# Layer 3 attention: stacked 64-row score matmuls, and one exponential in sixteen on VectorE

## The chip, the cores and the metric

The kernel runs on one core of a Trainium2 chip. The metric is device time in microseconds (us). TensorE is called PE here, its weight loads PEld, ScalarE is ACT, VectorE is DVE, GpSimd is POOL, and SP is the queue that issues the DMAs.

## What is computed

Four layers run over x of shape (2, 128, 64, 64), each `x = x + layer(groupnorm(x))`. Only the last one, attention over 4096 pixels with 8 heads of 16 channels, is changed:

```python
# layer 3, on xf = groupnorm(x) as (B=2, C=128, S=4096)
q, k, v = proj(wq, bq), proj(wk, bk), proj(wv, bv)      # each (B, 8, 16, S)
a = einsum('bhcq,bhck->bhqk', q, k) / sqrt(128)
a = softmax(a, axis=-1)
o = einsum('bhqk,bhck->bhcq', a, v).reshape(B, C, h, w)
x = x + o
```

## The kernel before, in words

Line numbers are those of the kernel before; a program prints the functions below. Layers 0 to 2 end at 2222 us of the trace and are not touched. Layer 3 (`_layer3`, L1963) works through four groups, one for each image b and half t of the heads: four heads at a time. A group has 8 query blocks (qb) of 512 queries, and a block has 32 key tiles (kt) of 128 keys. One (qb, kt) is called a step here; there are 4 x 8 x 32 = 1024.

In a step `scores` (L2102) multiplies keys by queries for the four heads. A head stands on 32 rows: 16 rows of rounded keys, 16 rows of what the rounding lost, and the queries twice (`q[0]` rounded, `q[1]` the rest). The first pass (n = 0) puts four matmuls of 32 rows side by side on the array, one for each head, and the second pass (n = 1) adds four more. Heads 0 and 1 fill one PSUM tile of two banks (p = 0), heads 2 and 3 another (p = 1). The pool has three such tiles (`spp`, bufs=3), used in turn. ACT then takes the exponential of each tile, 128 x 1024 (L2112), into an SBUF tile `weights`, of which there are eight. `multiply` (L2121) takes the weights of two steps earlier by the values, four matmuls of 128 rows and 32 columns, each recorded as two, and adds into a PSUM tile `ps_acc`, which there are two of. After the 32nd key tile `done` divides by the sum and adds the residual on DVE (L2144 to L2152), with four small DMAs for the residual (L2141) and four for the output (L2154).

Queries and keys of a group (L2030 to L2046) are made in eight chunks of 512 columns, values (L2056, L2063) in eight portions of four key tiles. `work` makes those of the next group as a generator, of which `attend` takes one piece at kt 4, 12 and 20 of each block; those of the first group are made during its own first block, one piece at every second step. So a side matmul stands in PE's queue between a step's multiply and the next step's scores. The instructions of PE, DVE, ACT and POOL keep the program's order (`_in_order`); SP's order is chosen by the scheduler. At the end of a group the two waiting steps are multiplied before the next group's first scores.

Of the kernel before, what the change touches and what calls it, by code (L numbers as in the profile page):

```python
# [10 lines left out]
F32 = mybir.dt.float32  # L11
# [1277 lines left out]
F32R = mybir.dt.float32r  # L1289
ENGINES = (  # L1290
# [672 lines left out]
def _layer3(ctx, tc, X, l3, cst, out, worst, here):  # L1963
# [6 lines left out]
    pp = ctx.enter_context(tc.tile_pool(name="f3_p", bufs=8))  # L1970
# [16 lines left out]
    def folded(b, got):  # L1987

        x = X[:, b, :]
        if b:  # L1990
            mean, rstd = _group_stats_pow(nc, two, acc, x, cst, mhalf)
        else:
            mean, rstd = here[:, 0:1], here[:, 1:2]
        yield
# [24 lines left out]
    def queries_and_keys(b, t, f, q, k, idle):  # L2019

        wqk, _, bqk, _ = f
        bq, bk, bk2 = (bqk[:, n, t : t + 1] for n in range(3))
        for c in range(NCH):
            cols = slice(c * CH, (c + 1) * CH)
            ps = acc()
            nc.tensor.matmul(ps, wqk[:, t, :], X[:, b, cols], start=True, stop=True)  # L2030

            qq = two.tile([128, CH], F32, tag="qq", name="qq", bufs=1)
            nc.vector.stream_shuffle(qq, ps, OF_Q)  # L2033
            kk = two.tile([128, CH], F32, tag="kk", name="kk", bufs=1)
            nc.vector.stream_shuffle(kk, ps, OF_K)  # L2035
            hi = two.tile([128, CH], F32R, tag="hi", name="hi", bufs=1)
            if c < idle:
                nc.scalar.activation(hi, kk, AF.Identity, bias=bk)
                nc.scalar.activation(kk, kk, AF.Identity, bias=bk2, scale=upper)  # L2039
                nc.scalar.activation(q[0][:, cols], qq, AF.Identity, bias=bq)  # L2040
            else:
                nc.vector.tensor_scalar_add(hi, kk, bk)
                nc.vector.tensor_scalar(kk, kk, bk, upper, ALU.add, ALU.mult)
                nc.vector.tensor_scalar_add(q[0][:, cols], qq, bq)
            nc.vector.scalar_tensor_tensor(k[:, cols], hi, sign, kk, ALU.mult, ALU.add)
            nc.vector.scalar_tensor_tensor(  # L2046
                q[1][:, cols], qq, bq, q[0][:, cols], ALU.add, ALU.subtract
            )
            yield
# [20 lines left out]
    def bound(b, t, q, k):  # L2070


        top = two.tile([128, 2, 2], F32, tag="top", name="top")
        for n, x in enumerate((q[0], k)):
            for i in range(2):
                nc.vector.tensor_reduce(
                    top[:, n, i : i + 1],
                    x[:, i * S // 2 : (i + 1) * S // 2],
                    AX.X,
                    ALU.max,  # L2080
                    apply_absolute_value=True,
                )
                yield
        m = two.tile([128, 2], F32, tag="m", name="m")
        nc.vector.tensor_reduce(m, top, AX.X, ALU.max)
# [4 lines left out]
        n = 1 + 2 * b + t  # L2090
        nc.vector.tensor_scalar_mul(worst[:, n : n + 1], ps[:, 0:1], 1.02)
        yield

    def attend(b, t, q, k, vt, early):
        ac = [None]

        def scores(qb, kt):
            ps = [spp.tile([128, 2, CH], F32, tag="sp", name="ps_s") for _ in range(2)]
            for n in range(2):
                for j in range(4):  # L2100
                    rows = slice(32 * j, 32 * j + 32)
                    nc.tensor.matmul(  # L2102
                        ps[j // 2][:, j % 2, :],
                        k[rows, kt * 128 : (kt + 1) * 128],
                        q[n][rows, qb * CH : (qb + 1) * CH],
                        start=(n == 0),
                        stop=(n == 1),
                    )
            w = []
            for p in range(2):  # L2110
                w.append(pp.tile([128, 2, CH], F32, tag="weights", name="weights"))
                nc.scalar.activation(w[p], ps[p], AF.Exp)  # L2112
            return w

        def multiply(qb, kt, w):
            if kt == 0:
                ac[0] = acc()
            for j in range(4):

                i = j % 2  # L2120
                nc.tensor.matmul(  # L2121
                    ac[0][32 * j : 32 * j + 32, :],
                    vt[:, kt, j // 2, i : i + 2, :].rearrange("p a d -> p (a d)"),
                    w[j // 2][:, i, :],
                    start=(kt == 0),
                    stop=(kt == NQT - 1),
                )
            if kt == NQT - 1:
                done(qb, ac[0])

        def done(qb, ps):
            cols = slice(qb * CH, (qb + 1) * CH)

            places = [
                (slice(32 * j + 16 * (j % 2), 32 * j + 16 * (j % 2) + 16),
                 slice(64 * t + 16 * j, 64 * t + 16 * j + 16))
                for j in range(4)
            ]
            xs = residual[qb % 2]
            for to, rows in places:  # L2140
                nc.sync.dma_start(xs[to, :], X[rows, b, cols])  # L2141
            z = two.tile([128, CH // 32, 32], F32, tag="z", name="z", bufs=1)
            flat = z.rearrange("p n i -> p (n i)")
            nc.vector.transpose(flat, ps)  # L2144
            r = two.tile([128, CH // 32], F32, tag="r", name="r")
            for j in range(4):
                rows = slice(32 * j, 32 * j + 32)
                nc.vector.reciprocal(r[rows, :], z[rows, :, 16 * (1 - j % 2)])  # L2148
            nc.vector.tensor_mul(z, z, r.unsqueeze(2).to_broadcast([128, CH // 32, 32]))
            u = two.tile([128, CH], F32, tag="u", name="u", bufs=1)  # L2150
            nc.vector.transpose(u, flat)
            nc.vector.tensor_add(u, u, xs)  # L2152
            for at, rows in places:
                nc.sync.dma_start(out[b, rows, cols], u[at, :])  # L2154

        waiting = []
        for qb in range(NCH):
            for kt in range(NQT):
                if kt % 2 == 0:
                    over = next(early, early) is early  # L2160
                waiting.append((qb, kt, scores(qb, kt)))
                if len(waiting) > 2:
                    multiply(*waiting.pop(0))
                yield kt if over else None
        for x in waiting:
            multiply(*x)
# [10 lines left out]
    def work():  # L2177

        for b in range(B):
            f = []  # L2180
            yield from folded(b, f)
            for t in range(2):
                first = b == 0 and t == 0
                q = [two.tile([128, S], F32R, tag=f"q{n}", name=f"q{n}") for n in range(2)]
                k = two.tile([128, S], F32R, tag="k", name="k")
                vt = two.tile([128, NQT, 2, 3, 16], F32, tag="vt", name="vt")
                early = values(b, t, f, vt)
                keys = queries_and_keys(b, t, f, q, k, 2 * first)
                if first:

                    for _ in range(2):
                        next(keys)
                        next(early)
                        yield
                    early = in_turn(keys, early)
                else:
                    for _ in early:
                        yield
                    yield from keys
                yield b, t, (q, k, vt, early)  # L2200
                yield from bound(b, t, q, k)

    def up_to_next(side):
        for x in side:
            if x:
                found.append(x)
                return
            yield

    side = work()  # L2210
    found = []
    for _ in up_to_next(side):
        pass
    while found:
        b, t, got = found.pop()
        beside = up_to_next(side)
        for kt in attend(b, t, *got):

            if kt in (4, 12, 20):
                next(beside, None)  # L2220
        for _ in beside:
            pass


def _input(nc, X, a, b):
    for i in range(4):
# [127 lines left out]
```

## Time and profile before

| what | us |
|---|---|
| time, median of 3 runs (lowest, highest) | 4194.57 (4191.61, 4198.47) |
| the profiled execution, its own time | 4192.35 |
| its span, first to last instruction | 4190.2 |
| first and last exponential of layer 3 begin | 2233.1, 4176.8 |
| ACT, busy in the span | 3333.8 (80%) |
| PE, busy in the span | 4027.6 (96%) |
| DVE, busy in the span | 2088.3 (50%) |

A group of instructions is shown as: line, engine, operation, out<-in, shape, count, then busy time and mean ns of one, then the idle time of the engine just before them with what ended it. Ends of matmuls are modelled and their records overlap (0.593 us each in L2121, the two halves of a multiply 0.454 us apart), so a PE row that is always busy may still wait between two records. An exponential's record likewise includes its latency: what counts is how far apart two starts are.

### The profile page before, as it was taken

What the parts mean: (1) busy time and instruction counts of PE and PEld (TensorE: products, weight loads), DVE (VectorE), ACT (ScalarE), POOL (GpSimd) and SP (SyncE); (2) the same over time, 40 slices, a digit from 0 to 9 for tenths busy, and PEclk for the clock granted to TensorE, in tenths of its full rate; (3) what the DMA queues carried; (4) which work ended last, traced back from release to release, by engine and by line L of the source; (5) the groups of instructions that cost most, each with busy time, mean ns of one, the idle gap of its engine ahead of it and who ended that gap; (6) DMA issues with size and microseconds to landing.
All of it is one profiled execution on the core that took longest, in us unless ns stands there. A gap on an engine that the chain in (4) does not pass through costs nothing. (4 is left out here: it accounts for less than half of the span.)

```text
span 4190.2 us, 90476 instructions
## 1 busy us (share of the span) xinstructions
PE 4027.6 (96%) x39886; PEld 1505.7 (36%) x39886; DVE 2088.3 (50%) x2454; ACT 3333.8 (80%) x4035; POOL 71.7 (2%) x145
## 2 busy tenths in 40 slices
PE   7999999989999998997999999999999999999998
PEld 4522222354222224445664333333333333333333
DVE  4689999767899998895754102221022102210000
ACT  4478888735888883326646999999999999999998
POOL 1001000000000001000000000000000000000000
PEclk9999999999999999998989999999999999999999
DMA  1199970000000000004640000000000000000000
GB/s 49 26 185 181 179 98 1 2 2 2 1 2 2 2 2 12 1 15 190 271 195 4 6 6 6 4 6 6 4 6 6 6 4 6 6 4 6 6 6 5
DMA packets 158855, 159.39 MB, mean 38 GB/s; under 512 B 24809, under 2 KB 148713, under 8 KB 154354
## 3 DMA queue, kind: packets, MB, share of 16 engines
q1 hardware_dynamic: 158450, 153.50, 15.7%
q8 instruction: 314, 5.14, 0.5%
q14 instruction: 91, 0.75, 0.1%
HBM read 145.09 MB, written 73.40 MB: 52 GB/s over the span
## 5 line engine op out<-in xcount | busy, mean ns | idle before, releaser
L2112 ACT ACTIVATE weights<-ps_s 128x1024 f32<-128x1024 f32 x2048 | 1884.9, 1101 | 61.0 <-PE ps_s L2102 60.6
L1352 ACT ACTIVATE weights<-ps_s 128x1024 f32<-128x1024 f32 x1024 | 993.1, 1023 | 167.9 <-PE ps_s L1343 149.7
L2121 PE MATMUL ps_acc<-weights,vt 128*32 128x512 f32 x8192 | 1093.2, 606 | 0.0
L2102 PE MATMUL ps_s<-q,k 32*128 32x512 f32 x8192 | 924.1, 444 | 5.4 <-ACT weights L2112 5.4
L1800 DVE TENSOR_TENSOR sums<-sums,weights 128x2048 f32<-128x2048 f32 x384 | 880.0, 2292 | 42.6 <-ACT weights L1352 6.4
L2102 PEld LDWEIGHTS ps_s<-q,k 32*128 32x128 f32 x8192 | 471.2, 182 | 839.7 <-ACT weights L2112 773.1
L1343 PE MATMUL ps_s<-q,k 32*64 32x512 f32 x8192 | 629.9, 613 | 4.6 <-ACT weights L1352 2.4
L1760 PE MATMUL ps_acc<-weights,vt 128*32 128x512 f32 x4096 | 550.0, 605 | 7.2 <-ACT used L1790 3.7
L2144 DVE STREAM_TRANSPOSE z<-ps_acc 128x512 f32<-128x512 f32 x32 | 22.9, 717 | 1064.6 <-PE ps_acc L2121 1064.6
L1343 PEld LDWEIGHTS ps_s<-q,k 32*64 32x64 f32 x8192 | 161.5, 129 | 433.9 <-PE ps_s L1343 337.9
L2121 PEld LDWEIGHTS ps_acc<-weights,vt 128*32 128x32 f32 x8192 | 162.9, 108 | 378.6 <-issue 375.4
L1760 PEld LDWEIGHTS ps_acc<-weights,vt 128*32 128x32 f32 x4096 | 81.2, 108 | 426.7 <-issue 403.2
L662 DVE SCALAR_TENSOR_TENSOR X<-g,w,X 128x2048 f32<-128x2048 f32 x84 | 197.4, 2351 | 2.6
L1800 DVE TENSOR_TENSOR sums<-weights 128x2048 f32<-128x2048 f32 x64 | 146.6, 2291 | 63.0 <-ACT weights L1352 62.6
L1548 PE MATMUL ps_sp<-pad,diag 32*32 32x512 f32 x4608 | 158.9, 597 | 2.3 <-ACT q L1568 1.3
L1008 PE MATMUL ps_z<-w_ri,e 128*32 128x128 f32 x2048 | 137.5, 409 | 14.5 <-DVE e L950 12.3
L2063 DVE TENSOR_TENSOR vt<-ps_acc,bv 128x384 f32<-128x384 f32 x32 | 17.8, 557 | 264.7 <-PE ps_acc L2056 264.7
L2033 DVE LOAD_MASK_SELECT qq<-ps_acc x32 | 0.4, 14 | 239.0 <-PE ps_acc L2030 239.0
L1548 PEld LDWEIGHTS ps_sp<-pad,diag 32*32 32x32 f32 x4608 | 95.5, 103 | 53.6 <-issue 15.6
L950 DVE TENSOR_SCALAR e<-ps_pe 32x136 f32<-32x136 f32 (+1 forms) x352 | 104.4, 297 | 4.9
L948 ACT ACTIVATE e<-ps_pe 32x136 f32<-32x136 f32 (+1 forms) x352 | 99.3, 282 | 4.1
L710 PE MATMUL ps_bank<-t,t 128*128 128x512 f32 x224 | 101.3, 610 | 0.0
(288 smaller groups left out, 2488.6 us busy)
## 6 DMA issues: line engine op xcount, KB each, us to landing
w_ri<-w_r SPq DMA_DIRECT2D x16, 2112.0 KB, 8.1
w_ri<-w_i SPq DMA_DIRECT2D x16, 2112.0 KB, 13.4
w_r<-in_L_conv_kr_w SPq DMA_DIRECT2D x15, 528.0 KB, 13.1
w_r<-in_L_conv_kr_x SPq DMA_DIRECT2D x15, 528.0 KB, 12.9
w_r<-in_L_conv_kr_y SPq DMA_DIRECT2D x15, 528.0 KB, 12.9
w_r<-in_L_conv_kr_z SPq DMA_DIRECT2D x15, 528.0 KB, 12.9
w_i<-in_L_conv_ki_w SPq DMA_DIRECT2D x15, 528.0 KB, 13.3
w_i<-in_L_conv_ki_x SPq DMA_DIRECT2D x15, 528.0 KB, 12.7
```

The costliest lines, as they stand in the source:

```text
L662: nc.vector.scalar_tensor_tensor(xi, g[:, i : i + H // 2, j : j + W], w8[:, s : s + 1], xi, ALU.mult, ALU.add)
L710: nc.tensor.matmul(ps.rearrange("p (h w) -> p h w", w=W), t9[:, k, :], t2[:, c * ROWS + k : (c + 1) * ROWS + k, 2 : W + 2], start=(k == 0) ...
L950: nc.vector.tensor_scalar_mul(out, got[of, :, s], sign)
L1008: nc.tensor.matmul(out.rearrange("p (n f o) -> p n f o", n=2, f=2), e[:, s, 2 * j : 2 * j + 2, :].rearrange("p f x -> p (f x)"), w.rearran ...
L1343: nc.tensor.matmul(ps[j // 2][to, j % 2, :], k[rows, kt * 128 + 64 * half : kt * 128 + 64 * half + 64], q[rows, qb * CH : (qb + 1) * CH], ...
L1352: nc.scalar.activation(w[:, 2 * p : 2 * p + 2, :], ps[p], AF.Exp)
L1548: nc.tensor.matmul(ps[r // 2][to, r % 2, :].rearrange("p (h w) -> p h w", w=W), diag[rows, grp, t, :], pad[rows, y0 : y0 + ROWS, t % 3 : t ...
L1760: nc.tensor.matmul(ac[n][rows, :], lhs(rows), w[:, j, :], start=first, stop=last)
L1800: nc.vector.tensor_add(parts[0].rearrange("p j c -> p (j c)"), t.rearrange("p j c -> p (j c)"), w.rearrange("p j c -> p (j c)"),)
L2102: nc.tensor.matmul(ps[j // 2][:, j % 2, :], k[rows, kt * 128 : (kt + 1) * 128], q[n][rows, qb * CH : (qb + 1) * CH], start=(n == 0), stop= ...
L2112: nc.scalar.activation(w[p], ps[p], AF.Exp)
L2121: nc.tensor.matmul(ac[0][32 * j : 32 * j + 32, :], vt[:, kt, j // 2, i : i + 2, :].rearrange("p a d -> p (a d)"), w[j // 2][:, i, :], star ...
```

## The change

A head's scores now stand on 64 rows. The queries and keys of a chunk are made as before, in tiles of one chunk (`qs0`, `qs1`, `ks`). They are stored to DRAM and loaded from there into stacks: `q[c]` with the rows of `q[0]` and `q[1]` alternating, `k[c]` with each key row twice. Each stack is a tile of its own for a chunk, of one buffer, and the next group's stack is loaded as soon as this group no longer needs the chunk. A chunk takes three stores and eight loads. The scores of a step are then four matmuls of 64 rows, two heads at a time.

Of the 64 exponentials of a block, the four with kt in (6, 13, 20, 27) and p = 1 go to DVE, as eight instructions of 128 x 1024 (`exponentials`), one portion issued ahead of each following step. Their weights are multiplied later, in place 12, 19, 26 and 31 (`BY_VECTOR`). All other weights are multiplied three steps late (`LAG`) instead of two, and the weights have 11 buffers. Groups no longer end with an empty queue: the waiting steps run on into the next group. Side pieces stand at kt 3, 6, 9, ... 30, in turn for `others` (values, statistics, bound) and `keys`, a quarter of a chunk each; the bound's reductions are taken chunk by chunk. The new functions, with what is left of the diff:

```diff
+LAG = 3
+SIDE = tuple(range(3, NQT, 3))
+BY_VECTOR = {(6, 1): 12, (13, 1): 19, (20, 1): 26, (27, 1): 31}
-    pp = ctx.enter_context(tc.tile_pool(name="f3_p", bufs=8))
+    pp = ctx.enter_context(tc.tile_pool(name="f3_p", bufs=11))
...
+        nc.vector.scalar_tensor_tensor(k, k, sign, kk, ALU.mult, ALU.add)
+        nc.vector.scalar_tensor_tensor(q[1], qq, bq, q[0], ALU.add, ALU.subtract)
+        for n, x in enumerate((q[0], q[1], k)):
+            to = dram.tile([128, CH], F32, name=f"stack{2 * b + t}_{c}_{n}")
+            nc.sync.dma_start(to, x.bitcast(F32))
+            g.kept[c, n] = to
+        yield
+        for n, x in enumerate((q[0], k)):
+            nc.vector.tensor_reduce(
+                top[:, n, c : c + 1], x, AX.X, ALU.max, apply_absolute_value=True
             )
...
+    def stacked(g, c, name, parts):
+        to = one.tile([128, 2, CH], F32R, tag=f"{name}{c}", name=f"{name}{c}")
+        for n, part in enumerate(parts):
+            for p in range(2):
+                nc.sync.dma_start(
+                    to[n::2, p, :].bitcast(F32), g.kept[c, part][64 * p : 64 * p + 64, :]
+                )
...
+    def exponentials(ps, out):
+        i = two.tile([128, 2 * CH], I32, tag="exp_i", name="exp_i", bufs=1)
+        nc.vector.tensor_scalar(
+            i, ps.rearrange("p j c -> p (j c)"), EXP_SCALE, EXP_BIAS, ALU.mult, ALU.add
+        )
+        yield
+        m = two.tile([128, 2 * CH], I32, tag="exp_m", name="exp_m", bufs=1)
+        nc.vector.tensor_scalar(
+            m, i, 0x7FFFFF, 0x3E800000, ALU.bitwise_and, ALU.bitwise_or
+        )
+        nc.vector.tensor_scalar(
+            i, i, 0x7F800000, 0x40000000, ALU.bitwise_and, ALU.bitwise_xor
+        )
+        yield
...
+        for n in EXP_TERMS[:-1]:
+            nc.vector.scalar_tensor_tensor(z, x, n, m, ALU.add, ALU.mult)
+            x = z
+            yield
+        w = pp.tile([128, 2, CH], F32, tag="weights", name="weights")
+        nc.vector.scalar_tensor_tensor(
+            w.rearrange("p j c -> p (j c)"), z, EXP_TERMS[-1], power, ALU.add, ALU.mult
+        )
...
-            for n in range(2):
-                for j in range(4):
-                    rows = slice(32 * j, 32 * j + 32)
-                    nc.tensor.matmul(
-                        ps[j // 2][:, j % 2, :],
-                        k[rows, kt * 128 : (kt + 1) * 128],
-                        q[n][rows, qb * CH : (qb + 1) * CH],
-                        start=(n == 0),
-                        stop=(n == 1),
-                    )
+        for j in range(4):
+            rows = slice(64 * (j % 2), 64 * (j % 2) + 64)
+            nc.tensor.matmul(
+                ps[j // 2][:, j % 2, :],
+                g.k[kt // 4][rows, j // 2, keys],
+                g.q[qb][rows, j // 2, :],
+                start=True,
+                stop=True,
+            )
+        for p in range(2):
+            g.weights[qb, kt, p] = w = []
+            if (kt, p) in BY_VECTOR:
+                chain[0] = exponentials(ps[p], w)
+                next(chain[0])
...
+        for n in range(NCH * NQT):
+            qb, kt = divmod(n, NQT)
+            if kt % 2 == 0:
+                over = next(early, early) is early
+            next(chain[0], None)
+            scores(g, qb, kt)
+            waiting.append((g, qb, kt))
+            if len(waiting) > LAG:
+                multiply(*waiting.pop(0))
+            if after:
+                laid(qb, kt)
+            if not over or kt not in SIDE:
+                continue
+            if SIDE.index(kt) % 2 == 0:
+                next(others, None)
+                continue
+            if after is None and following and qb:
+                for _ in others:
+                    pass
+                after, others = following()
+                keys = chained(*after.keys)
+            next(keys, None)
```

More of the change, by code (lines that the diff above doesn't have):

```diff
@@ L1289, with _order @@
 F32R = mybir.dt.float32r
+I32 = mybir.dt.int32
+EXP_SCALE = 2.0**23 / math.log(2.0)
+EXP_BIAS = -0.056912465706070565 * 2.0**23
+EXP_TERMS = (
+    -0.05306617170572281,
+    1.286389708518982,
+    0.8973912596702576,
+    0.7359788417816162,
+    0.25916776061058044,
+)
+LAG = 3
+SIDE = tuple(range(3, NQT, 3))
+BY_VECTOR = {(6, 1): 12, (13, 1): 19, (20, 1): 26, (27, 1): 31}
+def _order(pair):
+    order = [kt for kt in range(NQT) if (kt, pair) not in BY_VECTOR]
+    for (kt, p), at in BY_VECTOR.items():
+        if p == pair:
+            order.insert(at, kt)
+    return order
+ORDER = [_order(p) for p in range(2)]
 ENGINES = (
@@ L1962, in _layer3 @@
 @with_exitstack
-def _layer3(ctx, tc, X, l3, cst, out, worst, here):
+def _layer3(ctx, tc, X, l3, cst, out, worst, here, dram):
     nc = tc.nc
@@ L1985, in _layer3, with folded @@
         nc.gpsimd.memset(r, 0.0)
[L1987 to L1994, printed above, removed]
+    def folded(b, st, got):
+        mean, rstd = st[:, 0:1], st[:, 1:2]
         wqk = two.tile([128, 2, 128], F32, tag="wqk", name="wqk", bufs=1)
@@ L2017, in folded, with queries_and_keys @@
         yield
-    def queries_and_keys(b, t, f, q, k, idle):
-        wqk, _, bqk, _ = f
+    def queries_and_keys(g, c, idle):
+        b, t, top = g.b, g.t, g.top
+        wqk, _, bqk, _ = g.f
         bq, bk, bk2 = (bqk[:, n, t : t + 1] for n in range(3))
[L2027 to L2047, printed above, removed]
-            )
-            yield
@@ new lines, in queries_and_keys @@
+        cols = slice(c * CH, (c + 1) * CH)
+        ps = acc()
+        nc.tensor.matmul(ps, wqk[:, t, :], X[:, b, cols], start=True, stop=True)
+        qq = two.tile([128, CH], F32, tag="qq", name="qq", bufs=1)
+        nc.vector.stream_shuffle(qq, ps, OF_Q)
+        kk = two.tile([128, CH], F32, tag="kk", name="kk", bufs=1)
+        nc.vector.stream_shuffle(kk, ps, OF_K)
+        yield
+        k = two.tile([128, CH], F32R, tag="ks", name="ks", bufs=1)
+        q = [two.tile([128, CH], F32R, tag=f"qs{n}", name=f"qs{n}", bufs=1) for n in range(2)]
@@ new lines, in queries_and_keys @@
+        if idle:
+            nc.scalar.activation(k, kk, AF.Identity, bias=bk)
+            nc.scalar.activation(kk, kk, AF.Identity, bias=bk2, scale=upper)
+            nc.scalar.activation(q[0], qq, AF.Identity, bias=bq)
+        else:
+            nc.vector.tensor_scalar_add(k, kk, bk)
+            nc.vector.tensor_scalar(kk, kk, bk, upper, ALU.add, ALU.mult)
+            nc.vector.tensor_scalar_add(q[0], qq, bq)
+        yield
+        nc.vector.scalar_tensor_tensor(k, k, sign, kk, ALU.mult, ALU.add)
@@ L2051, in values @@
+    def stacked(g, c, name, parts):
[5 more added lines that the diff above has]
+                )
+        getattr(g, name)[c] = to
     def values(b, t, f, vt):
@@ L2068, in values, with bound @@
             yield
[L2070 to L2081, printed above, removed]
-                )
-                yield
+    def bound(g):
         m = two.tile([128, 2], F32, tag="m", name="m")
-        nc.vector.tensor_reduce(m, top, AX.X, ALU.max)
+        nc.vector.tensor_reduce(m, g.top, AX.X, ALU.max)
         mm = two.tile([128, 1], F32, tag="mm", name="mm")
@@ L2089, in bound @@
         nc.tensor.matmul(ps[:, 0:1], head_sum, mm, start=True, stop=True)
-        n = 1 + 2 * b + t
+        n = 1 + 2 * g.b + g.t
         nc.vector.tensor_scalar_mul(worst[:, n : n + 1], ps[:, 0:1], 1.02)
         yield
[L2094 to L2098, printed above, removed]
-            for n in range(2):
-                for j in range(4):
-                    rows = slice(32 * j, 32 * j + 32)
-                    nc.tensor.matmul(
-                        ps[j // 2][:, j % 2, :],
-                        k[rows, kt * 128 : (kt + 1) * 128],
-                        q[n][rows, qb * CH : (qb + 1) * CH],
-                        start=(n == 0),
-                        stop=(n == 1),
-                    )
-            w = []
-            for p in range(2):
-                w.append(pp.tile([128, 2, CH], F32, tag="weights", name="weights"))
[L2112 to L2166, printed above, removed]
@@ new lines, in exponentials @@
+    def exponentials(ps, out):
[3 more added lines that the diff above has]
+        )
+        yield
+        m = two.tile([128, 2 * CH], I32, tag="exp_m", name="exp_m", bufs=1)
[5 more added lines that the diff above has]
+        )
+        yield
+        m, power = m.bitcast(F32), i.bitcast(F32)
+        z = two.tile([128, 2 * CH], F32, tag="exp_z", name="exp_z", bufs=1)
+        x = m
+        for n in EXP_TERMS[:-1]:
+            nc.vector.scalar_tensor_tensor(z, x, n, m, ALU.add, ALU.mult)
+            x = z
+            yield
+        w = pp.tile([128, 2, CH], F32, tag="weights", name="weights")
+        nc.vector.scalar_tensor_tensor(
+            w.rearrange("p j c -> p (j c)"), z, EXP_TERMS[-1], power, ALU.add, ALU.mult
+        )
+        out.append(w)
+        yield
@@ new lines, in _layer3, with __init__ @@
+    class Group:
+        def __init__(self, b, t, f, idle=0):
+            self.b, self.t, self.f, self.ac = b, t, f, None
+            self.kept, self.q, self.k = {}, {}, {}
+            self.vt = two.tile([128, NQT, 2, 3, 16], F32, tag="vt", name="vt")
+            self.top = two.tile([128, 2, NCH], F32, tag="top", name="top")
+            self.keys = [queries_and_keys(self, c, c < idle) for c in range(NCH)]
+            self.values = values(b, t, f, self.vt)
+            self.weights = {}
+    chain = [iter(())]
@@ new lines, in scores @@
+    def scores(g, qb, kt):
+        ps = [spp.tile([128, 2, CH], F32, tag="sp", name="ps_s") for _ in range(2)]
+        keys = slice(kt % 4 * 128, kt % 4 * 128 + 128)
+        for j in range(4):
[6 more added lines that the diff above has]
+                stop=True,
+            )
+        for p in range(2):
[3 more added lines that the diff above has]
+                next(chain[0])
+            else:
+                w.append(pp.tile([128, 2, CH], F32, tag="weights", name="weights"))
+                nc.scalar.activation(w[0], ps[p], AF.Exp)
@@ new lines, in multiply @@
+    def multiply(g, qb, at):
+        if at == 0:
+            g.ac = acc()
+        for j in range(4):
+            i, kt = j % 2, ORDER[j // 2][at]
+            (w,) = g.weights[qb, kt, j // 2]
+            nc.tensor.matmul(
+                g.ac[32 * j : 32 * j + 32, :],
+                g.vt[:, kt, j // 2, i : i + 2, :].rearrange("p a d -> p (a d)"),
+                w[:, i, :],
+                start=(at == 0),
+                stop=(at == NQT - 1),
+            )
+        if at == NQT - 1:
+            done(g.b, g.t, qb, g.ac)
@@ new lines, in done @@
+    def done(b, t, qb, ps):
+        cols = slice(qb * CH, (qb + 1) * CH)
+        places = [
+            (slice(32 * j + 16 * (j % 2), 32 * j + 16 * (j % 2) + 16),
+             slice(64 * t + 16 * j, 64 * t + 16 * j + 16))
+            for j in range(4)
+        ]
+        xs = residual[qb % 2]
+        for to, rows in places:
+            nc.sync.dma_start(xs[to, :], X[rows, b, cols])
+        z = two.tile([128, CH // 32, 32], F32, tag="z", name="z", bufs=1)
+        flat = z.rearrange("p n i -> p (n i)")
+        nc.vector.transpose(flat, ps)
+        r = two.tile([128, CH // 32], F32, tag="r", name="r")
+        for j in range(4):
+            rows = slice(32 * j, 32 * j + 32)
+            nc.vector.reciprocal(r[rows, :], z[rows, :, 16 * (1 - j % 2)])
+        nc.vector.tensor_mul(z, z, r.unsqueeze(2).to_broadcast([128, CH // 32, 32]))
+        u = two.tile([128, CH], F32, tag="u", name="u", bufs=1)
+        nc.vector.transpose(u, flat)
+        nc.vector.tensor_add(u, u, xs)
+        for at, rows in places:
+            nc.sync.dma_start(out[b, rows, cols], u[at, :])
@@ L2175, in in_turn @@
                     yield
[L2177 to L2207, printed above, removed]
-            yield
[L2210 to L2221, printed above, removed]
-            pass
+    def in_pieces(gen, n):
+        while True:
+            for _ in range(n):
+                if next(gen, gen) is gen:
+                    return
+            yield
@@ new lines, in chained, with run, attended, laid @@
+    def chained(*gens):
+        for g in gens:
+            yield from g
+    def run(gen):
+        for _ in gen:
+            pass
+    waiting = []
+    def attended(g, early, others, following):
+        after, over, keys = None, False, iter(())
+        def laid(qb, kt):
+            for name, parts, free in (("q", (0, 1), qb), ("k", (2, 2), kt // 4 if qb == NCH - 1 else 0)):
+                c = len(getattr(after, name))
+                if c < free and (c, 2) in after.kept:
+                    stacked(after, c, name, parts)
+        for n in range(NCH * NQT):
[20 more added lines that the diff above has]
+            next(keys, None)
+        if after:
+            run(keys)
+            run(others)
+            for name, parts in (("q", (0, 1)), ("k", (2, 2))):
+                for c in range(len(getattr(after, name)), NCH):
+                    stacked(after, c, name, parts)
+        return after
@@ new lines, in first_laid, with following @@
+    def first_laid(keys, g):
+        for c in range(NCH):
+            yield from keys[c]
+            stacked(g, c, "q", (0, 1))
+            stacked(g, c, "k", (2, 2))
+    f = []
+    run(folded(0, here, f))
+    g = Group(0, 0, f, 2)
+    keys = in_pieces(first_laid(g.keys, g), 4)
+    for c in range(2):
+        next(keys)
+        next(g.values)
+    early = in_turn(keys, g.values)
+    second = two.tile([128, 2], F32, tag="second", name="second", bufs=1)
+    for b in range(B):
+        for t in range(2):
+            others, following = bound(g), None
+            if t == 0:
+                def following():
+                    x = Group(b, 1, f)
+                    more = iter(())
+                    if b + 1 < B:
+                        more = _stats_steps(nc, two, acc, X[:, b + 1, :], cst, mhalf, second)
+                    return x, chained(x.values, more)
+            elif b + 1 < B:
+                f = []
+                others = chained(others, folded(b + 1, second, f))
+                def following():
+                    x = Group(b + 1, 0, f)
+                    return x, x.values
+            g = attended(g, early, others, following)
+            early = iter(())
@@ L2225, in _input @@
+    run(chain[0])
+    for x in waiting:
+        multiply(*x)
 def _input(nc, X, a, b):
@@ L2283 @@
                 )
-            _layer3(tc, X, l3, cst, out, worst, st[:, B + 1])
+            _layer3(tc, X, l3, cst, out, worst, st[:, B + 1], dram)
         with tc.tile_pool(name="flag_ps", bufs=1, space=PSUM) as fp:
```

## The prediction, on record before the changed kernel ran

> **What bounds the kernel now.** I read the groups of the page first, for the costliest lines of layer 3.
>
> ```profile
> PE 4027.6 (96%) x39886; PEld 1505.7 (36%) x39886; DVE 2088.3 (50%) x2454; ACT 3333.8 (80%) x4035; POOL 71.7 (2%) x145
> ...
> L2112 ACT ACTIVATE weights<-ps_s 128x1024 f32<-128x1024 f32 x2048 | 1884.9, 1101 | 61.0 <-PE ps_s L2102 60.6
> ...
> L2121 PE MATMUL ps_acc<-weights,vt 128*32 128x512 f32 x8192 | 1093.2, 606 | 0.0
> L2102 PE MATMUL ps_s<-q,k 32*128 32x512 f32 x8192 | 924.1, 444 | 5.4 <-ACT weights L2112 5.4
> ...
> L2102 PEld LDWEIGHTS ps_s<-q,k 32*128 32x128 f32 x8192 | 471.2, 182 | 839.7 <-ACT weights L2112 773.1
> ```
>
> PE looks full, but its loads for the scores wait 773 us for the exponentials, and ACT waits only 61 us, in 68 places, for PE. Next the busy time by window: a block with three side pieces, then one without.
>
> ```profile
> 2481.00:2543.00 62.00, 62.00 (x546) 22.66 (x544) 5.47 (x11) 59.43 (x66) 0.00 (x0) 1.00 0.02 5
> ...
> 3884.00:3943.00 59.00, 59.00 (x520) 20.16 (x514) 3.79 (x8) 59.00 (x65) 0.00 (x0) 1.00 0.03 6
> ```
>
> The columns are PE, PEld, DVE, ACT. Without side pieces ACT is busy throughout. By the starts of the exponentials such a block takes 58.67 us, 0.917 for each of 64; one with three side pieces 61.54. DVE is nearly idle. Last, the timeline of one step, and of a step after a side matmul.
>
> ```profile
> 3850.58 0.47 PEld L2102 LDWEIGHTS ps_s<-q,k 32*128 32x128 f32 x8 [0.84 <-ACT weights L2112]
> ...
> 3851.42 0.16 PEld L2121 LDWEIGHTS ps_acc<-weights,vt 128*32 128x32 f32 x8 [0.37 <-issue]
> ...
> 3852.42 0.18 PEld L2102 LDWEIGHTS ps_s<-q,k 32*128 32x128 f32 x2 [0.84 <-ACT weights L2112]
> ```
>
> ```profile
> 3502.33 0.30 PEld L2102 LDWEIGHTS ps_s<-q,k 32*128 32x128 f32 x8 [0.76 <-ACT weights L2112]
> ...
> 3503.00 0.16 PEld L2121 LDWEIGHTS ps_acc<-weights,vt 128*32 128x32 f32 x8 [0.37 <-issue]
> ```
>
> Scores take 0.84 us where PE waits for a tile and 0.67 where both tiles are free, multiply 1.00. So PE needs 1.67 a step where ACT needs 1.83: ACT bounds a block, with PE 9% behind it, and a side matmul (1.05 us) costs ACT 0.96.
>
> **The loop between the two.** From the records of that step: exponentials last 1.117 us from start to end. When one ends, the loads into its tile begin 0.05 later. Passes on the same rows are 0.335 apart, of which 0.10 is the first weight load, so a further pass is 0.235. From the start of p = 1's first pass to the next step's p = 0 is 1.66; p = 0's first pass to the end of its second is 0.73; the exponential follows 0.10 later. Sum: 0.05 + 1.66 + 0.73 + 0.10 = 2.54. ACT wants that tile 4 x 0.917 - 1.117 = 2.55 after. There is no slack at all, though each engine alone has some.
>
> **64-row scores.** No row shows 64 rows. Nearest is L2102 with 32: neighbours start some 4 ns apart, so tiles run side by side. If two 64-row tiles do too, a step is two rounds on the same rows, as before, and PE's 1.67 stays. What goes is latency: p = 1 waits for its tile before one pass and not two (1.66 - 0.235 = 1.42), and p = 0 is complete after one (0.49). The loop becomes 0.05 + 1.42 + 0.49 + 0.10 = 2.06, 0.49 to spare. Alone this moves a block without side pieces by nothing: ACT's 58.67 stays. The bounds: four matmuls at half the price of eight would take another 0.2 off the step, which ACT hides; one after another, see the rivals.
>
> **A rule against it.** The Trainium skill ("TensorE: Matmul & The Clock Gate", Part 3, The mechanism) says that a weight load overlaps a matmul in flight only if it is for other rows. Heads 2 and 3 now use the rows of heads 0 and 1, so their load would come after the stream: 0.10 more a step, 1.77, or 56.6 us a block against the 56.7 below. Side matmuls would then cost their full 0.96 to 1.05, and my sum would be some 15 us higher. But the records show the second pass's loads, for the same rows, at 3850.764, inside the first pass's stream, and its matmul at 0.335. I go by the row.
>
> **Exponentials on DVE.** Four of 64 leave ACT: 0.917 each. But PE can run only three tiles ahead. In the loop above, with (i, 1) gone ACT wants step i+2's first tile after 3 x 0.917 - 1.117 = 1.63, and it comes after 2.06: 0.43 is lost, 0.49 gained. Per block 4 x 0.49 = 1.95, 58.67 to 56.7. ACT idles 1.7 a block in front of scores; PE, at 32 x 1.67 = 53.4, keeps 3.3. On 31 blocks: **-60 us**. The bounds are 0 (nothing gets through the three tiles) and 31 x 4 x 0.917 = 114.
>
> DVE's price: one read of PSUM, 1.225 (L1559, a copy of 128x1024); two bitwise steps, 0.75 (L1689, a scalar operation of 128x1024) to 1.28 if they run as slowly as a two-tensor one; five of two tensors, 1.28 (between 0.746 for 512 in L2045 and 2.351 for 2048 in L662). Sum 9.1 to 10.2 us, portion by portion over seven steps of 1.77, 12.4. In a block DVE has 4 x 9.3 = 37, `done` 3.8 (L2144 to L2152), 1.25 chunks of keys at 5.9 and values 1: 49 of 56.7. It fits. Behind each portion stand the side pieces' shuffles (1.5 us) and `done`; behind them the next read of PSUM, for which step i+2's scores wait. The read may come about 1.2 us late before it costs; `done` is over two steps before kt 6.
>
> **One stream, side pieces.** Blocks 2 to 32 hold 1876.7 - 31 x 58.67 = 58 us of stalls: some 17 side matmuls in each of three groups at 0.96, and 3 us at each group's end. The ends go. The matmuls stay, now against 0.49 of slack in an ordinary step and none just after a DVE exponential: between 0.5 and 0.96 each, I take 0.75, 51 x 0.75 = 38. **-20 us**, between -32 and -9.
>
> **The first block** gets slower. Chunk 0 leaves DVE at 2228.1. Then three stores (0.47 each on SP, as 128-row DMAs were issued) and a landing (2.3, as loads of 96 to 128 KB took 1.9 to 3.3), eight loads 0.63 apart (as L2141's), and a landing: 10 us. First scores near 2238 and not 2231.9: +7. In the block DVE owes 6.4 for each chunk with its values (L2033 to L2063, and two reductions of 0.68), 6 x 6.4 = 38, and ahead of the last chunk two exponentials, 19: from 2232 to 2289, with waits for PE near 2296. Ten more for the DMAs, four more steps: the block ends near 2318 and not 2301. **+18 us**; +8 if DVE packs tighter, +40 if a 64-row load issues at 1.2 us.
>
> Later groups' DMAs are hidden: 11 for a chunk are 7 us of SP in 45, and a stack is loaded most of a block ahead. SP's loads for the last block wait for PE's last use, with outputs and residuals behind them; `done` has a block for those. Cover gone, a late stack costs about 10 us a group. Tail: a step more in the queue, +1.
>
> **Sum**: -60 - 20 + 18 + 1 = -61 from the profiled 4192.35, its span and the 2 us around it alike: 4131. That execution lies 2.2 under the median 4194.57, so 4133.
>
> **The rivals.**
> *The matmuls of 64 rows don't run side by side* (the slower end). Scores then take 0.10 + 4 x 0.235 + 0.11 and a step 2.15, PE-bound: 1024 x 2.15 + 51 x 1.05 is 2255 for 1945, near 4500. It decides from a score section of 0.83. The 4 ns between neighbours speak against it, that no row has 64 rows for it. 0.07.
> *DVE becomes the bound.* If its instructions run a third longer, beside ACT on PSUM or with waits between dependent ones, 49 becomes 65 in the blocks with keys, the tile is held and PE waits for DVE: 20 such blocks at 60 and more, near 4180. ACT's pitch is the same 0.91 to 0.92 where DVE is busy as where it is idle, which speaks against. 0.15.
> *All of ACT's relief gets through*, PE being ahead more than I think: 1.7 less in 31 blocks, 4080. The slack of three tiles speaks against. 0.12.
> *As forecast*, 4105 to 4165 by the bounds of side pieces and first block: 0.66.
>
> The range holds the forecast and reaches to the two neighbours: 4078 to 4182. A measurement can tell about 0.2%, 8 us, from no change: faster 0.87, same 0.05 (DVE case), slower 0.08 (serial, and the worst of DVE).
>
> **What would show it.** Score matmuls in pairs 4 ns apart, pairs 0.34 apart; blocks of the last group near 56.7 by the starts of exponentials; ACT idle about 0.43 two steps after each DVE exponential; DVE chains of 9 to 10 us; first block's end near 2318; score loads waiting for DVE little. Wrong: a step over 1.83 everywhere, DVE above 90% in a block, or a last group at 55.

## The result, and the profile after

The changed kernel takes 4124.32 us (median of four, 4119.48 to 4130.53) against 4195.78 for the kernel before (median of four, 4191.61 to 4198.47): a ratio of 0.9831, 95% interval 0.9814 to 0.9848. The profiled execution took 4122.99, which is 69.4 under the profiled 4192.35 of before; its span is 4121.1, 69.1 under 4190.2. The forecast was 61 under. Line numbers from here on are those of the changed kernel; in the view of an experiment they are those of its own kernel, a few lines off.

First the engines and the groups of the page after, in the form of those shown for before.

```profile
PE 3944.4 (96%) x35790; PEld 1382.1 (34%) x35790; DVE 3183.8 (77%) x3526; ACT 3228.6 (78%) x3907; POOL 72.2 (2%) x145
...
L2181 ACT ACTIVATE weights<-ps_s 128x1024 f32<-128x1024 f32 x1920 | 1780.6, 1078 | 93.8 <-PE ps_s L2167 93.7
...
L2167 PE MATMUL ps_s<-q,k 64*128 64x512 f32 x4096 | 838.4, 472 | 6.3 <-DVE exp_i L2123 3.0
L2167 PEld LDWEIGHTS ps_s<-q,k 64*128 64x128 f32 x4096 | 352.7, 184 | 948.4 <-ACT weights L2181 824.7
...
L2139 DVE SCALAR_TENSOR_TENSOR exp_z<-exp_z,exp_m 128x1024 f32<-128x1024 f32 x384 | 469.7, 1223 | 11.2
L2123 DVE TENSOR_SCALAR exp_i<-ps_s 128x1024 int32<-128x1024 f32 x128 | 156.7, 1224 | 254.0 <-PE ps_s L2167 253.1
```

ACT has lost 128 of 2048 exponentials and 104 us of busy time, but waits 94 us for PE where it waited 61. PE was and is "96% busy": that figure says nothing of the change. DVE went from 50% to 77%, and in this row PE's matmuls wait only 3 us for it. The windows show the cover that DVE has left, in a block with side pieces and in one without (PE, PEld, DVE, ACT).

```profile
2311.50:2373.00 61.50, 61.50 (x424) 20.24 (x420) 43.95 (x58) 55.96 (x62) 0.00 (x0) 1.00 0.09 27
3826.00:3882.00 56.00, 56.00 (x386) 16.16 (x384) 38.14 (x41) 55.21 (x61) 0.00 (x0) 1.00 0.03 6
```

By the starts of the exponentials, a block without side pieces takes 56.25 (58.67 before). Where the 69.4 come from:

| term | forecast | measured |
|---|---|---|
| quiet pace, 31 blocks (58.67 to 56.25) | -60 | 31 x -2.42 = -75.0 |
| stalls over the quiet pace in blocks 2 to 32 (57.9 to 52.4) | -20 | -5.5 |
| first exponential (2233.1 to 2236.9) and first block (68.14 to 74.57) | +18 | +10.2 |
| last exponential's start to the end (13.37 to 14.56) | +1 | +1.2 |
| sum | -61 | -69.1 |

The total is nearer than its two largest terms, whose errors, -15 and +14.5, point opposite ways; that is luck. The experiments ask why.

### The profile page after: what moved, and what is told of

Same layout as the page of the kernel before. It is cut to its first block, busy times and chain, and to the rows that moved or that the text cites. A ratio compares the mean times of both kernels' runs of the same rounds, so it can differ in the third digit from the quotient of the medians.

```text
span 4121.1 us, 83188 instructions
## 1 busy us (share of the span) xinstructions
PE 3944.4 (96%) x35790; PEld 1382.1 (34%) x35790; DVE 3183.8 (77%) x3526; ACT 3228.6 (78%) x3907; POOL 72.2 (2%) x145
## 5 line engine op out<-in xcount | busy, mean ns | idle before, releaser
L2181 ACT ACTIVATE weights<-ps_s 128x1024 f32<-128x1024 f32 x1920 | 1780.6, 1078 | 93.8 <-PE ps_s L2167 93.7
L1379 ACT ACTIVATE weights<-ps_s 128x1024 f32<-128x1024 f32 x1024 | 992.9, 1023 | 169.3 <-PE ps_s L1370 151.1
L2167 PE MATMUL ps_s<-q,k 64*128 64x512 f32 x4096 | 838.4, 472 | 6.3 <-DVE exp_i L2123 3.0
L2167 PEld LDWEIGHTS ps_s<-q,k 64*128 64x128 f32 x4096 | 352.7, 184 | 948.4 <-ACT weights L2181 824.7
L2139 DVE SCALAR_TENSOR_TENSOR exp_z<-exp_z,exp_m 128x1024 f32<-128x1024 f32 x384 | 469.7, 1223 | 11.2
L2123 DVE TENSOR_SCALAR exp_i<-ps_s 128x1024 int32<-128x1024 f32 x128 | 156.7, 1224 | 254.0 <-PE ps_s L2167 253.1
L2143 DVE SCALAR_TENSOR_TENSOR weights<-exp_z,exp_i 128x1024 f32<-128x1024 f32 x128 | 156.7, 1224 | 13.9
L2139 DVE SCALAR_TENSOR_TENSOR exp_z<-exp_m 128x1024 f32<-128x1024 f32 x128 | 155.9, 1218 | 0.0
L1008 PE MATMUL ps_z<-w_ri,e 128*32 128x128 f32 x2048 | 137.4, 409 | 14.5 <-DVE e L950 12.4
L2213 DVE STREAM_TRANSPOSE z<-ps_acc 128x512 f32<-128x512 f32 x32 | 22.9, 717 | 104.1 <-PE ps_acc L2190 104.1
```

The lines of the kernel that those rows point to most:

```text
L1379: nc.scalar.activation(w[:, 2 * p : 2 * p + 2, :], ps[p], AF.Exp)
L2123: nc.vector.tensor_scalar(i, ps.rearrange("p j c -> p (j c)"), EXP_SCALE, EXP_BIAS, ALU.mult, ALU.add)
L2139: nc.vector.scalar_tensor_tensor(z, x, n, m, ALU.add, ALU.mult)
L2143: nc.vector.scalar_tensor_tensor(w.rearrange("p j c -> p (j c)"), z, EXP_TERMS[-1], power, ALU.add, ALU.mult)
L2167: nc.tensor.matmul(ps[j // 2][:, j % 2, :], g.k[kt // 4][rows, j // 2, keys], g.q[qb][rows, j // 2, :], start=True, stop=True,)
L2181: nc.scalar.activation(w[0], ps[p], AF.Exp)
```

## Experiments

The first four ran on one chip beside nine runs of the kernel before (median 4195.54), the last three beside nine more (4190.03); ratios are to these. The intervals of e3, e4, e5 and e6 overlap that of the changed kernel, so what they show is read from block lengths in the traces: quiet blocks of the changed kernel and of e3 to e7 agree to 0.03 us. Block lengths are taken from the starts of the first exponentials. In the first expectation, Theory A is one I formed after the result from the starts of the exponentials, that an exponential takes ACT 0.9035 and not 0.917; Theory B keeps the prediction's loop.

**e1, without the exponentials on DVE**: the 64 rows and the one stream alone.

```diff
-BY_VECTOR = {(6, 1): 12, (13, 1): 19, (20, 1): 26, (27, 1): 31}
+BY_VECTOR = {}
```

> All 64 exponentials of a block on ACT again; stacks, 64-row scores and the one stream stay. Theory A (formed from the trace after): ACT's own pitch is 0.9035 us, and before the change a quiet block was held at 58.67 by the loop between PE and ACT, not by ACT alone. Then 64 rows alone bring a quiet block of the last group to 64 x 0.9035 = 57.8, and the time lies 31 x 1.57 = 49 above the changed kernel, less some 6 for a first block that DVE no longer delays: 4165. Theory B (the prediction's own step): ACT's pitch is 0.917, 64 rows alone move a quiet block by nothing, 58.67, and the time is some 31 x 2.42 - 6 = 69 above: 4192.

Measured: 4172.78, ratio 0.9948 (0.9934 to 0.9962), and a quiet block of 58.67, exactly as before the change. First the window of such a block, then the durations of the exponentials (min, median, max in ns) in this run, then in the kernel before:

```profile
3922.00:3981.00 59.00, 59.00 (x390) 17.17 (x386) 3.79 (x8) 59.00 (x66) 0.00 (x0) 1.00 0.02 5
```

```profile
L2181 ACT ACTIVATE weights<-ps_s x2048: 1017/1392/1592, 2234.3 to 4156.3; 128x1024 f32<-128x1024 f32 x187
```

```profile
L2112 ACT ACTIVATE weights<-ps_s x2048: 1018/1117/1130, 2233.1 to 4176.8; 128x1024 f32<-128x1024 f32 x187
```

The block is unmoved while the records in it grow from 1.117 to 1.58: PE runs further ahead, so a record's length includes waiting. After a stall the records start 0.9035 apart and each is 0.013 longer than the one before; their ends are 0.9165 apart in every kernel here. Theory A had read the starts, and falls. Theory B has the block right and the time, 4192, wrong: it kept the changed kernel's stalls in blocks 2 to 32, 52.4, and here they are 35.5. Against the 57.9 of before, the stream and the unspent slack of the tile loop save 22, where 20 was forecast.

**e2, exponentials on DVE with the scores left on 32 rows.** The later multiply (`LAG` 3) and the 11 weight buffers are those of the changed kernel. To make room, the queries have one buffer and a group's side pieces run between the groups, so only the quiet blocks are read and not the time (4312.01, one run).

```diff
-            nc.scalar.activation(w[p], ps[p], AF.Exp)
...
+            if (kt, p) in BY_VECTOR:
+                chain[0] = exponentials(ps[p], w)
+                next(chain[0])
...
-        for kt in attend(b, t, *got):
-            if kt in (4, 12, 20):
-                next(beside, None)
+        for _ in attend(b, t, *got):
+            pass
```

> The kernel before, 32-row scores, with four exponentials of a block on DVE. To make room in SBUF the queries have one buffer and the side pieces stand between the groups and not beside the blocks, so only blocks 2 to 8 of each group are read, by the starts of the exponentials, not the whole time. Theory A: the loop of the kernel before has no slack, so an exponential taken from ACT only makes ACT wait: a quiet block stays at 58.4 to 58.7, with ACT idle 0.8 to 0.9 after each DVE exponential. Rival: the relief comes through without the 64 rows: 57 or less.

Measured: a quiet block of 58.1, 0.57 under before's, though ACT has 3.67 less to do in it. The timeline of ACT around one exponential on DVE:

```profile
4239.16 1.12 ACT L2174 ACTIVATE weights<-ps_s 128x1024 f32<-128x1024 f32 x1
4240.99 5.61 ACT L2174 ACTIVATE weights<-ps_s 128x1024 f32<-128x1024 f32 x6 [0.71 <-PE ps_s L2160]
```

ACT stands idle 0.71 for scores; by the records' ends it is 0.76 (1.68 from end to end, for a pitch of 0.9165), and nearly the same four times a block. The block lies below the 58.4 of Theory A and far above the 57 of its rival. So neither half does it: the 64 rows alone give a quiet block 0, DVE alone 0.57, both 2.42. One opens a slack, the other has the use for it.

**e3, the first block's exponentials on ACT.**

```diff
-            if (kt, p) in BY_VECTOR:
+            if (kt, p) in BY_VECTOR and not first_block(g, qb):
...
-            i, kt = j % 2, ORDER[j // 2][at]
+            i, kt = j % 2, (PLAIN if first_block(g, qb) else ORDER)[j // 2][at]
```

> The changed kernel, but in the very first block all exponentials are on ACT. Theory A (as in the prediction): DVE owes keys, values and exponentials in that block, and its backlog holds the key stacks; the first block falls from 74.6 to 66 to 69 us and the time by 5 to 9: about 4117. Rival: the chain of stores and loads on SP sets that block: 74 stays, and the time moves by less than 2.

Measured: 4117.46 (0.981, 0.9796 to 0.9823); the first block takes 68.16 where it took 74.57, and 68.14 before the change. The two first blocks, changed kernel and this one, in PE, PEld, DVE, ACT:

```profile
2236.90:2311.50 74.60, 66.77 (x426) 24.05 (x430) 67.48 (x104) 56.62 (x61) 0.00 (x0) 0.95 0.52 169
```

```profile
2234.90:2303.00 68.10, 67.74 (x426) 24.43 (x430) 33.99 (x72) 59.59 (x64) 0.00 (x0) 0.93 0.56 185
```

DVE is busy 67.5 of 74.6 in the one and 34.0 of 68.1 in the other. The exponentials on DVE cost this block 6.4; the DMAs through the stacks cost it nothing once it has begun. ACT stands idle 19.7 in the changed kernel's first block and 9.7 in this one's. The two longest waits are 3.3 at kt 28, shown here, and 2.9 at kt 15, where PE waits 3.9 for DVE to read the tile of kt 13:

```profile
2300.38 1.23 DVE L2143 SCALAR_TENSOR_TENSOR weights<-exp_z,exp_i 128x1024 f32<-128x1024 f32 x1
2301.71 1.23 DVE L2123 TENSOR_SCALAR exp_i<-ps_s 128x1024 int32<-128x1024 f32 x1
...
2303.04 0.22 DVE L2113 SCALAR_TENSOR_TENSOR mm<-m,lower 128x1 f32<-128x1 f32 x1
...
2303.41 0.35 PE L2115 MATMUL ps_acc<-mm,head_sum 128*128 128x1 f32 x2 [2.68 <-DVE mm L2113]
...
2304.24 4.69 ACT L2181 ACTIVATE weights<-ps_s 128x1024 f32<-128x1024 f32 x5 [3.23 <-PE ps_s L2167]
```

The exponential of kt 27 reads its tile late, behind the chain of kt 20; behind that read stands the operand of the first group's bound, and PE waits for it ahead of the next scores. So it is DVE's queue that is full here, and what stands behind what counts as much as the sum of the work.

**e4, the next group's bound later**: its small matmul at kt 9 and not at kt 3 of the block.

```diff
     def bound(g):
+        yield
```

> The changed kernel with the bound of a group taken at kt 9 and not at kt 3 of the next group's first block. Theory A: its small matmul L2115 stands in PE's queue while DVE is still in done, and PE and then ACT stand still for 2.4 us, and the three steps behind it run late; at kt 9 DVE is free. The first blocks of groups 2 to 4 fall from 60.3-61.2 to about 57, the time by 9 to 12: about 4113. Rival: the wait only moves, since DVE is as busy at kt 9 with an exponential: less than 4.

Measured: 4112.91 (0.9803, 0.9787 to 0.9819). The first blocks of groups 2 to 4 go from 61.17, 60.33 and 60.26 to 57.44, 56.24 and 56.25. This is the wait that I had not foreseen, in the timeline of the changed kernel at the second group's start:

```profile
2723.27 0.72 DVE L2213 STREAM_TRANSPOSE z<-ps_acc 128x512 f32<-128x512 f32 x1 [4.28 <-PE ps_acc L2190]
...
2726.55 0.69 DVE L2221 TENSOR_TENSOR u<-u,residual 128x512 f32<-128x512 f32 x1
...
2727.36 0.22 DVE L2113 SCALAR_TENSOR_TENSOR mm<-m,lower 128x1 f32<-128x1 f32 x1
...
2727.73 0.35 PE L2115 MATMUL ps_acc<-mm,head_sum 128*128 128x1 f32 x2 [2.69 <-DVE mm L2113]
...
2728.61 1.02 ACT L2181 ACTIVATE weights<-ps_s 128x1024 f32<-128x1024 f32 x1 [2.38 <-PE ps_s L2167]
```

`done` of the last block (L2213 to L2221) fills DVE; the bound's 0.22 us stands behind it; its matmul of one column stands in PE's queue ahead of the next step's scores; PE waits 2.69 and ACT 2.38. The three steps behind it lose another 1.5 to 1.6 together, and with them a group change costs the 3.7 to 4.1 that the move saves. With the matmul at kt 9, ACT works through the same `done` without a wait:

```profile
2718.88 14.78 ACT L2182 ACTIVATE weights<-ps_s 128x1024 f32<-128x1024 f32 x16
...
2727.03 0.72 DVE L2214 STREAM_TRANSPOSE z<-ps_acc 128x512 f32<-128x512 f32 x1 [4.28 <-PE ps_acc L2191]
...
2730.30 0.69 DVE L2222 TENSOR_TENSOR u<-u,residual 128x512 f32<-128x512 f32 x1
```

The first group's bound, which the changed kernel takes at the end of block 1, stands in this run at kt 3 of block 2, again behind `done`: ACT waits 2.55 for it, and block 2 goes from 61.46 to 64.02. ACT's wait at kt 28 of the first block falls from 3.3 to 0.3, yet that block does not get shorter (75.47): its waits at kt 4 and 16 are 1.4 and 1.7 longer, for which I have no cause.

**e5, a shorter chain on DVE.** Four terms of the polynomial are left out, so its weights aren't exponentials.

```diff
-        x = m
+        z = m
         for n in EXP_TERMS[:-1]:
-            nc.vector.scalar_tensor_tensor(z, x, n, m, ALU.add, ALU.mult)
-            x = z
             yield
```

> The changed kernel with the four terms of the polynomial left out, so that a DVE exponential is four instructions (3.9 us) and not eight (9.0); the weights it makes are not exponentials. Theory: beside the first block DVE's work is hidden, and ACT's 0.30 us of idling at each DVE exponential comes from PE and the three tiles; quiet blocks stay at 56.25, the first block falls by about 6, group changes and side blocks by 0 to 5 in all: 4113 to 4120. Rival (DVE bounds the blocks, or its queue holds the tile): quiet blocks fall below 56, the time below 4100.

**e6, a longer one**: the read of PSUM issued twice.

```diff
+        nc.vector.tensor_scalar(
+            i, ps.rearrange("p j c -> p (j c)"), EXP_SCALE, EXP_BIAS, ALU.mult, ALU.add
+        )
```

> The changed kernel, but DVE reads each score tile from PSUM twice (1.22 us more before the tile comes free, 4.9 us of DVE a block). Theory, by the loop: DVE's read begins when the scores are there and ends about when ACT has done the tile before; the next scores into that tile come 1.4 us later, so 1.22 fits in a quiet block: 56.25 to 56.6. In blocks with side pieces DVE's queue is fuller and the tile comes late: 5 to 15 us in all, with the first block 4129 to 4142. Rival (the read is already what PE waits for): every quiet block grows by 4 x 0.6 or more, to 58.6, and the time by 70.

Measured: 4112.85 (0.9818, 0.9803 to 0.9833) and 4128.87 (0.9859, 0.9844 to 0.9874). A quiet block, first of the short chain, then of the long one:

```profile
3830.00:3886.00 56.00, 56.00 (x388) 16.20 (x384) 18.93 (x24) 55.19 (x61) 0.00 (x0) 1.00 0.03 6
```

```profile
3842.00:3898.00 56.00, 56.00 (x384) 16.09 (x381) 43.27 (x44) 55.21 (x61) 0.00 (x0) 1.00 0.03 6
```

DVE is busy 18.9 and 43.3 us, and the blocks take 56.25 and 56.24. Between a third and three quarters of its time, DVE's work costs a quiet block nothing, and the blocks with side pieces are the changed kernel's too (the second of a group 61.39 to 61.45): of the 5 to 15 us expected for e6 there, nothing shows (the two runs' first blocks of groups 2 to 4 are 58.7 to 61.5). The first block takes 71.59 and 84.92 (74.57 in the changed kernel). e5's 3.0 are half of what was expected, although DVE is busy 48.6 in it and not 67.5; e6's 10.3 are twice the 4.9 that it adds to DVE. Both agree with a queue in which a late read holds a tile, and not with a bare sum of DVE's work; the block's waits were not separated further.

**e7, both mends.** The first block's exponentials on ACT, and the bound at kt 9 in all groups but the first.

```diff
     def bound(g):
+        if g.b or g.t:
+            yield
...
+            if (kt, p) in BY_VECTOR and not first_block(g, qb):
```

> The changed kernel with the first block's exponentials on ACT and the bound at kt 9 for all groups but the first. If the two mends are independent, the first block is 68 and the first blocks of groups 2 to 4 are 56.3 to 57.4: 6.4 and 11.8 less, about 4106. Rival: they share a wait (SP or DVE in the first group), and only the larger shows: 4112.

Measured: 4102.87 (median of five, 4098.14 to 4104.03), ratio 0.9795 (0.9782 to 0.9808): ahead of both kernels. Against the changed kernel the span falls by 22.7: 5.5 in the first block (69.08), 11.8 at the group changes (57.45, 56.24, 56.25), and 5.6 because the first exponential starts at 2231.3 and not 2236.9. This last is not the edit's: layers 0 to 2, which it doesn't touch, end 6.5 earlier in this execution (last write at 2214.5 and not 2221.0). Stalls of 40.8 in blocks 2 to 32 are left, nearly all of side matmuls.

## Why the prediction was right, and where its terms were not

**64-row scores, forecast nothing in a quiet block: right.** e1's 58.67 shows it. The rival of serial matmuls is refuted: from the records, the two matmuls of a pair start mostly 3 to 4 ns apart and the pairs 0.33 to 0.34 apart where the tiles are free. The Trainium skill's rule ("TensorE: Matmul & The Clock Gate", Part 3, The mechanism) would have loads for the same rows wait for the stream; the same section lets loads into a background weight buffer run ahead, which I had left out. In the timeline after, two steps behind an exponential on DVE:

```profile
3838.56 2.86 ACT L2181 ACTIVATE weights<-ps_s 128x1024 f32<-128x1024 f32 x3 [0.25 <-PE ps_s L2167]
...
3839.79 0.30 PEld L2167 LDWEIGHTS ps_s<-q,k 64*128 64x128 f32 x4 [0.84 <-DVE exp_m L2128]
...
3840.45 0.16 PEld L2190 LDWEIGHTS ps_acc<-weights,vt 128*32 128x32 f32 x8 [0.37 <-issue]
```

All four loads are over 0.30 after the first began, and those of heads 2 and 3 began 0.108 after those of heads 0 and 1, on the same rows and inside their stream. A free score section is 3840.45 - 3839.79 = 0.66; by the rule it would be 0.10 more. The row was the better guide; whether a background buffer is the reason, no run here shows.

**Exponentials on DVE, forecast -60, measured -75: the mechanism right, one term mis-sized.** The mis-sized term is the 0.43 that ACT loses in each, in "ACT wants step i+2's first tile after 3 x 0.917 - 1.117 = 1.63, and it comes after 2.06". The 1.117 is the length of a record that has waited. An exponential that ACT stands idle for starts fresh and lasts 1.02 (the 2.86 of three above is 1.02 and two pitches of 0.92), so its tile is wanted after 1.73 and comes after 2.06: 0.33. Measured by ends, ACT's gap is 1.215 for a pitch of 0.9165, 0.30 lost (the first of four in a block 0.36); the page's 0.25 counts from a record's start. Then 4 x 0.9165 - 3 x 0.30 - 0.36 = 2.41 a block for the 2.42 measured. The place was off by a step as well: ACT idles before the first exponential of step i+1, not i+2. In the timeline above it is the one at 3838.56. Its scores come so late because PE, in step i, had waited for the tile that the exponential of (i-1, 0) sets free; that one ended 2.08 ahead of it.

The same 1.117 made "there is no slack at all" circular. In a quiet block without exponentials on DVE a record is as long as the loop leaves it: 4 x 0.9165 - 2.55 = 1.117 before, and 4 x 0.9165 - 2.08 = 1.59 with 64 rows, where e1's records level off at 1.58. Setting the loop against that length had to give nothing. Against a fresh record of 1.02 the kernel before had 0.10 to spare, and 64 rows have 0.57, not 0.49. e2 agrees: its loop of 2.54 would lose 2.54 - (3 x 0.9165 - 1.02) = 0.81 for each exponential on DVE, which is near the 0.76 measured and leaves some relief.

**One stream, forecast -20, measured -6: a term left out.** The pauses did go: no group's first exponential waits. But "the ends go" put the group change at nothing. There the bound's matmul now waits for DVE, 11.8 over three groups, shown by e4, where the ends had cost 9. I had costed the side pieces' matmuls, and of the bound none, though it issues one too. The side matmuls were sized well: about 41, 0.8 each, for 38 and 0.75. What I counted only in part is that the slack is spent once. In e1, less the same 11.8, they cost about 24; in its block 2 each costs 0.50 to 0.55. In block 2 of the changed kernel one costs 1.05 to 1.07 in the step of an exponential on DVE or the next, 0.88 two steps behind it and 0.55 three. e5 and e6 have the same to 0.02, so it is the tile loop that they wait for and not DVE's busy time: what DVE's exponentials take, side matmuls lose.

**The first block, forecast +18, measured +10: right in kind.** First scores came at 2236.1 for my 2238, the last chunk left DVE at 2292.3 for my 2296, the block ended at 2311.5 for 2318. DVE packed tighter, toward the +8 that I named; and the forecast's own parts, 2296, ten for the DMAs and four steps, add to 2313 and not 2318. e3 shows that the exponentials on DVE are all of the block's 6.4. The other 3.8 is the later start, and 3.4 of it is the way through the stacks: from the last write ahead of layer 3 to the first exponential 12.45 pass before the change (2220.68 to 2233.13), 15.87 after it (2221.03 to 2236.90), and 15.8 to 16.9 in the six experiments with stacks. The forecast had +7.

**DVE's cover: right.** A chain is 8.65 us of work in a quiet block (the 1224 and 1223 ns of the page after, 0.69 for each bitwise step), a little under the 9.1 to 10.2, and 8.95 from its first start to its last end. The rival "DVE becomes the bound" shows in the first block alone: DVE is busy 38.1 of 56 in a quiet block, and e6 adds 5 to that and nothing to the block's time. The rival "all of ACT's relief gets through" is refuted by 56.25 for 55.0.

## What to carry to other kernels

Read a loop over tiles from end to end, with the duration of a fresh record, before adding up what an engine is relieved of: relief counts only as far as the tiles let the feeding engine run ahead, and a slack pays for one use. When work is moved into a stream, follow its smallest instructions through every in-order queue: a matmul of one column held PE for 2.7 us because its operand stood behind 4 us of another job on DVE. And look for the stage where the newly loaded engine has no idle time; the same edit that paid 2.4 us in each quiet block cost 6.4 in the first.

## What was not expected of the hardware

ACT's records of one kind and shape (exponentials, 128 x 1024) last from 1.01 to 1.59 us at an unchanged pitch of 0.9165. After a wait the first lasts about 1.02; each one behind it starts 0.9035 after the one before and lasts 0.013 longer, until the length levels off, at 1.117 in the kernel before and 1.58 in e1. So while lengths change the pitch shows in the ends and not, as I said ahead of the prediction, in the starts, and a mean duration tells of the queue rather than of the work.
